# A two-layer graph network on one core: the second group's input is transposed a stage earlier, and its operand sums move to GpSimd

## The chip, the cores and the metric

One core of one Trainium2 chip runs the whole program. The metric is the device time of one execution in microseconds; a kernel's time is the median of its runs. Five engines work in order, each through its own list of instructions, and meet at semaphores: TensorE (PE in the profile; its weight loads are PEld), VectorE (DVE), ScalarE (ACT), GpSimd (POOL) and SyncE (SP), which issues all the DMAs of this kernel.

## The reference

`x` is 128 batches of 128 nodes with 512 features, `adj` a 128x128 matrix, all in float32. Two layers follow each other, a graph convolution and a masked attention with 8 heads, each on a normalised, rectified input and each added to its input.

```
h = max(layernorm(x), 0)
x = x + norm_adj @ (h @ weight) + bias          # norm_adj = adj scaled by its row sums
h = max(layernorm(x), 0)
q, k, v = h @ Wq + bq, h @ Wk + bk, h @ Wv + bv   # 8 heads of 64
scores = q k^T / 8 + (1 - adj) * -1e9
x = x + (softmax(scores) v) @ Wo + bo
```

## The kernel before

**Groups and slots.** The 128 batches are worked on in 32 groups of four (`GB = 4`, `NG = 32`). Time is cut into slots t = 0, 1, 2, ... In slot t, after a hand-written prologue, five products of 512x512 weights follow each other on PE, each called by a letter: W (the convolution weight of group t+1), Q, K and V of group t, and Y (the output weight of group t-1). So the first slot has Q, K, V of group 0 alone, and the slot after it W of group 2, Q, K, V of group 1 and Y of group 0. This document is about V of slot 0 to V of slot 1.

**A product.** The rows of a product are the 512 rows of a group, cut into a 2x2 of blocks like the weight. Seven block products take the place of eight (a Strassen-Winograd form), so a letter has seven steps, 0 to 6. Their left operands are A11, A12, S1, A22, S2, S3, S4; A11, A12, S1 and A22 are first written as the four blocks of the input, and `Operands.combine` (L381 to L384) forms S3, S1, S2 and S4 from them: four 128x512 additions, one after the other. From group 1 on, each of three or four block products is again done by seven smaller ones ("inner"), for which `combine_one` (L94) does nine further 128x256 additions on the operand, and nine on the weight. Three operand tiles exist: `op_a` (op_mix), `op_h` (op_norm) and `op_o` (op_att). The four banks of PSUM `a`, `d`, `b`, `c` hold the block products. Step 0 and 3 write bank a, step 1 bank d, step 2 bank b, step 4 banks b and d, step 5 bank a, step 6 banks b and c; two pieces of bank c are left over for steps 1 and 2 of the next letter. DVE (L448, L463) and ACT (L788, L802) read the banks out, and PE can't write a bank again before that.

**The plan.** What is not one of these products is placed by hand: `at(slot, place, function, ...)` says ahead of which step ("Q1"), after its first part ("Q1b") or after both parts ("Q1c") a piece of work is issued. The order in the program is the order on each engine, so a place decides what stands in front of what on every engine that the piece uses.

**The pieces that matter here.** `norm_h` (L351, ACT) normalises a batch, `transpose_h` turns it by 16 short PE matmuls (L742) and copies the result into the operand (L743, ACT); half 0 of a group (batches 0 and 1) fills A11 and A12, half 1 fills S1 and A22. `attention_operands` is `Operands.combine` on `op_h`. For attention, `row_max` (L850, DVE), `exponentials` (L858, ACT, four or eight heads a call) and `softmax_end` (L865 on DVE, then L870 on POOL, or L868 on ACT for batches 2 and 3 of group 0) follow each other; batch 3 gets its mask apart by `add_mask` (L846, POOL). `split_att` (L875, ACT) writes an attention matrix as two planes of 16-bit words into the buffer of the batch before it and sends it to memory (L876, SP), `turn_att` (L879, SP) brings it back transposed; `transpose_att` does the same on PE (L886). `ln1` and `gcn_norm` prepare the convolution input of group 3 in slot 1 (statistics L332/L333 on DVE, scale L337 to L340 on POOL, L351 on ACT), and `gcn_mix` multiplies it by the graph matrix on PE (`pa`).

**The first round of the weights.** In slots 0 and 1 the weights' own sums are made on POOL and written to memory for later slots (`keep_w`, L205, SP). The value weight lies in the tile `op_o` for that time. Its sums end in slot 1; then it is written out, then the output weight is loaded into the same tile (`load_w`, L201), summed (L282, L94) and written out, and only then may the attention output of group 0 be copied into the tile (L908, ACT). From slot 2 on weights only come back from memory.

The two entries of the plan that say which engine sums the operand of group 1, and which softmax step uses which engine, read:

```
op_h[g].combine(nc.vector if g < 2 else nc.gpsimd, g > 0, within=nc.gpsimd)
if g == 1 or g == 0 and b >= 2:   # ACT, else POOL
```

Of the kernel before, what the change touches and what calls it, by code (L numbers as in the profile page):

```python
# [97 lines left out]
def kernel(  # L98
# [16 lines left out]
    nc = tc.nc  # L115
    B, N, D = x.shape
    P = 128
    H = 8
# [3 lines left out]
    NG = B // GB  # L122
# [269 lines left out]
    op_mix, op_norm, op_att = (Operands(f"op_{k}") for k in "aho")  # L392
# [249 lines left out]
    scale1, op_a, op_h, op_o = {}, {}, {}, {}  # L642
# [123 lines left out]
        nc.sync.dma_start_transpose(out=blocks, in_=h_dram[half].rearrange("n z f -> (n z) f"))  # L766

    def attention_operands(g):
        op_h[g].combine(nc.vector if g < 2 else nc.gpsimd, g > 0, within=nc.gpsimd)

    def attention_residual(g, half):
        add_bias(xts[g, half], bo_bc, engine=nc.gpsimd if g else nc.vector)
# [153 lines left out]
    def at(slot, place, f, *args):  # L926
        plan.setdefault((slot, place), []).append((f, *args))

    for t in range(-1, NG + 1):
# [3 lines left out]
        if 0 <= t - 1 < NG - 1:  # L933
            g = t - 1

            for first, final, place, f, *args in (
                ("W1", "-Y6", "W5", turn_att, 0),
                ("W4b", "-Y6b", "W1b", split_att, 1),
                ("W5", "-Y3", "W2", exponentials, 2, 0, H // 2),
                ("W6", "-Y4", "W3", exponentials, 2, H // 2, H),  # L940
                ("Q2c", "-Y5b", "W4b", softmax_end, 2),
                ("Q1", "-Y5", "W5", exponentials, 3, 0, H // 2),
                ("Q2", "-Y6", "W6", exponentials, 3, H // 2, H),
                ("Q0", "Q1", "Q0", turn_att, 1),
                ("Q4b", "Q0b", "Q0b", softmax_end, 3),
                ("Q4b", "Q0b", "Q3b", split_att, 2),
                ("Q6b", "Q2", "Q5b", split_att, 3),
                ("K1", "Q2", "K0", turn_att, 2),
                ("K3", "Q5", "K2", turn_att, 3),
            ):  # L950
                place = first if t == 1 else final if last else place
                if f in (split_att, turn_att) and turned_in_place(g, args[0]):
                    continue
                at(t - place.startswith("-"), place.strip("-"), f, g, *args)
            if t == 1:
                at(1, "K3", transpose_att, g, 2)
                at(1, "K5", transpose_att, g, 3)
            elif last:
                at(t, "K1", transpose_att, g, 3)
            for b in (2, 3, 0, 1):  # L960
                at(t, "V0", attend, g, b)
        if t == 0:

            at(0, "Q0b", ln2, 1, 0)
            at(0, "Q1b", ln2, 1, 1)
            at(0, "K6", norm_h, 1, 0)
            at(0, "K6", norm_h, 1, 1)
            at(1, "W0", transpose_h, 1, 0)
            at(1, "W0", norm_h, 1, 2)
            at(1, "W1", transpose_h, 1, 1)  # L970
            at(1, "W1", norm_h, 1, 3)
            at(1, "W2", transpose_h, 1, 2)
            at(1, "W3", transpose_h, 1, 3)
            at(1, "W4b", attention_operands, 1)
            at(2, "Q5", attention_residual, 1, 0)
            at(2, "K1", attention_residual, 1, 1)
        elif 1 <= t + 1 < NG and t >= 0:
            g = t + 1
            at(t, "K0b" if g < NG - 1 else "Q0b", ln2, g, 0)
            at(t, "K6b" if g < NG - 1 else "Q3b", ln2, g, 1)  # L980
            if g == NG - 1:

                places = ("Q3", "Q4", "Q5", "Q5", "Q6", "Q6", "K1", "K2", "K2")
                steps = ((norm_h, 0), (norm_h, 1), (transpose_h, 0), (norm_h, 2), (transpose_h, 1), (norm_h, 3))
                steps += ((transpose_h, 2), (transpose_h, 3))
            else:
                places = ("K6", "K6", "V0b", "V1c", "V1c", "V2", None, None, "Y5")
                steps = ((norm_h, 0), (norm_h, 1), (norm_h, 2), (norm_h, 3), (split_h, 2), (split_h, 3))
                for half in range(2):
                    at(t, ("V1", "V2b")[half], write_h, g, half)  # L990
                    at(t, ("V5", "Y1b")[half], turn_h, g, half)
            for place, (f, b) in zip(places, steps):
                at(t, place, f, g, b)
            at(t, places[8], attention_operands, g)
            at(t + 1, "Q3", attention_residual, g, 0)
            at(t + 1, "Q4", attention_residual, g, 1)
# [6 lines left out]
        if 2 <= t + 2 < NG:  # L1003
            g = t + 2
# [11 lines left out]
        if 0 <= t < NG:  # L1016
            g = t
            for b in (0, 1, 3, 2):
                at(t, "V0", scores, g, b)
            if t > 0:  # L1020
                at(t, "V0", output_operands, t - 1)
                for b in range(2 if t < NG - 2 else 0):
                    at(t, "V0", split_h, t + 1, b)
            at(t, "V1b", row_max, g, 0)
            at(t, "V3b", exponentials, g, 0, 0, H // 2)
            at(t, "V4b", exponentials, g, 0, H // 2, H)
            at(t, "V6", softmax_end, g, 0)
            if last:
                at(t, "V5b", row_max, g, 1)
                at(t, "V5b", exponentials, g, 1, 0, H // 2)  # L1030
                at(t, "V6", exponentials, g, 1, H // 2, H)
                at(t, "Y1b", softmax_end, g, 1)
                at(t, "Y2", transpose_att, g, 0)
                at(t, "Y4", transpose_att, g, 1)
            else:
                if t > 0:
                    at(t, "V3b", row_max, g, 1)
                    at(t, "Y1", exponentials, g, 1, 0, H // 2)
                    at(t, "Y2", exponentials, g, 1, H // 2, H)
                    at(t, "Y4", softmax_end, g, 1)  # L1040
                else:
                    at(t, "V4b", row_max, g, 1)
                    at(t, "V5b", exponentials, g, 1, 0, H // 2)
                    at(t, "V6", exponentials, g, 1, H // 2, H)
                    at(t + 1, "W1b", softmax_end, g, 1)
                at(*((t, "Y3b") if t > 0 else (1, "W1")), split_att, g, 0)
                at(t, "V6b", row_max, g, 2)
                at(*((t, "Y1") if t > 0 else (1, "W0")), add_mask, g, 3)
                at(*((t, "Y3b" if g == NG - 2 else "Y6b") if t > 0 else (1, "W6b")), row_max, g, 3)
        if last:  # L1050
            g = t
            at(t, "Y0", row_max, g, 2)
# [64 lines left out]
    def prologue():  # L1117
# [64 lines left out]
        at(0, "K2", keep_w, "q")  # L1182
        at(0, "V1", combine_inner, "v", nc.gpsimd, range(4))
        at(0, "V5", combine_inner, "v", nc.gpsimd, (4, 5))
        at(1, "W0", combine_inner, "v", nc.gpsimd, (6, 7, 8))
        at(1, "W0", keep_w, "v")
        at(1, "W0", load_w, "o", wo, op_att.t)
        at(0, "V0", combine_inner, "k", nc.gpsimd)
        at(1, "Q3c", combine_w, "o", nc.gpsimd)
        at(1, "Q5", combine_inner, "o", nc.gpsimd)  # L1190
        at(1, "K3", keep_w, "o")
        at(1, "W0", output_bias)
        at(1, "K1c", attention_residual, 0, 0)
        at(1, "K2c", attention_residual, 0, 1)

# [66 lines left out]
```

## Time and profile before

| What | us |
|---|---|
| median of 3 runs (2200.32 to 2201.76) | 2201.11 |
| the profiled execution | 2200.75 |
| its span, first to last instruction | 2199.0 |
| PE busy | 2186.2 |
| POOL busy | 1886.1 |
| DVE busy | 1774.9 |
| ACT busy | 1393.8 |

The profiled execution's time is 1.75 us more than its span, and 0.36 us under the median. In the profile's windows of 55 us PE is busy for 52.11, 51.65 and 53.24 us in the first three, and for the whole of each one from 165 us to 2100 us; the last 99 us have 94.18. The granted clock is 0.97 in the window from 55 to 110 us and 1.00 in all others. In the timeline of PE, V of slot 0 begins at 74.96 us, W of slot 1 at 89.27, Q at 105.40, K at 121.01, the attention products at 137.05, V at 144.41 and Y at 155.10.

A line of a timeline has the start in us, the length in us, engine, line of the code, operation, output tile and input tiles, shapes and count, and in brackets the idle time before it with the instruction that ended it. Lengths overlap a little from one instruction to the next, so the distance between starts is what a row costs in a run of such rows.

### The profile page before, as it was taken

The page shows a single profiled execution, that of the slowest core. Times are in us where ns is not written, and L with a number is a line of the kernel's source. Part 1 is how long each engine was busy: PE and PEld are TensorE (multiplying, and loading weights), DVE is VectorE, ACT ScalarE, POOL GpSimd, SP SyncE. Part 2 cuts the span into 40 slices and gives each one's busy share as a digit, 9 for nine tenths or more (in the row PEclk, how much of TensorE's full clock was granted, in tenths as well). Part 3 has the DMA queues.
Part 4 walks back from the last instruction along what each step waited for, and adds up shares of the span by engine and source line. Part 5 has one row for each costly group of instructions (what it writes and reads, how often), then busy time and mean ns, then how long its engine had stood idle before and what let it go on. Part 6 is the DMA issues. An engine that isn't in the chain of part 4 may idle for free.

```text
span 2199.0 us, 77713 instructions
## 1 busy us (share of the span) xinstructions
PE 2186.2 (99%) x31749; PEld 1879.6 (85%) x31749; DVE 1774.9 (81%) x4244; ACT 1393.8 (63%) x3604; POOL 1886.1 (86%) x2049
## 2 busy tenths in 40 slices
PE   9999999999999999999999999999999999999999
PEld 7788888888888888888888888888888888888887
DVE  7777888878888778888788887788877888878876
ACT  4577665765666666666656676566666565765654
POOL 7988988898889898888988898888889888998754
PEclk9999999999999999999999999999999999999999
DMA  5489999999999999999999999999999999999982
GB/s 165 173 260 289 290 293 292 256 284 307 263 288 287 259 297 280 293 296 244 294 312 262 294 271 269 302 286 276 290 259 289 293 279 298 263 276 298 263 261 84
DMA packets 530613, 595.48 MB, mean 271 GB/s; under 512 B 389073, under 2 KB 396369, under 8 KB 529745
## 3 DMA queue, kind: packets, MB, share of 16 engines
q1 hardware_dynamic: 530256, 590.50, 90.6%
q8 instruction: 251, 4.11, 0.8%
q14 instruction: 106, 0.86, 0.1%
HBM read 358.68 MB, written 137.89 MB: 226 GB/s over the span
## 4 chain that ended last, share of the span: by engine, by line
PE 97%; DVE 1%; issue 0%; POOL 0%; DMA 0%; ACT 0%; SPq 0%; POOLq 0%; DVEq 0%; ACTq 0%
PE bank_a L140 37%; PE bank_d L140 22%; PE bank_b L140 11%; PE bank_c L140 11%; PE pa L140 5%; PE bank_d L831 3%; PE po L901 3%; PE pss L831 1%; PE bank_b L901 1%; PE bank_a L901 1%; PE bank_b L831 1%; PE paT L886 0%; DMA xt<-in_x_dram 0%; DVE xt L448 0%; POOL w L282 0%
## 5 line engine op out<-in xcount | busy, mean ns | idle before, releaser
L858 ACT ACTIVATE att<-att,nmx 128x128 f32<-128x128 f32 x1024 | 396.1, 393 | 0.5 <-DVE nmx L850 0.5
L140 PE MATMUL bank_a<-op_h,w 128*64 128x256 f32 x2976 | 353.5, 380 | 0.0
L870 POOL TENSOR_TENSOR att<-att,rsm 128x1024 f32<-128x1024 f32 x122 | 231.7, 1900 | 110.8 <-DVE rsm L865 98.3
L875 ACT COPY att<-att 128x2048 uint16<-128x2048 uint16 x121 | 229.2, 1894 | 114.6 <-POOL att L870 114.5
L448 DVE TENSOR_TENSOR xt<-xt,bank_d 128x512 f32<-128x512 f32 x610 | 270.3, 468 | 11.0 <-PE bank_d L140 0.5
L140 PEld LDWEIGHTS bank_a<-op_h,w 128*64 128x64 f32 x2976 | 207.9, 137 | 81.6 <-issue 0.5
L140 PE MATMUL bank_d<-op_h,w 128*64 128x128 f32 (+1 forms) x3424 | 221.7, 275 | 0.1
L94 POOL TENSOR_TENSOR op_o<-op_o 128x256 f32<-128x256 f32 x297 | 212.4, 739 | 10.1
L788 ACT ACTIVATE q<-bank_a,bqk 128x256 f32<-128x256 f32 x192 | 79.8, 466 | 211.5 <-PE bank_a L140 211.3
L94 POOL TENSOR_TENSOR op_a<-op_a 128x256 f32<-128x256 f32 x279 | 198.5, 734 | 9.6
L94 POOL TENSOR_TENSOR op_h<-op_h 128x256 f32<-128x256 f32 x270 | 191.2, 733 | 11.5 <-DVE op_h L384 2.1
L140 PEld LDWEIGHTS bank_d<-op_h,w 128*64 128x64 f32 x3424 | 195.0, 137 | 7.1 <-POOL w L282 0.5
L858 ACT ACTIVATION_READ_ACCUMULATOR att<-att,nmx 128x1 f32 x1024 | 196.6, 192 | 0.0
L140 PE MATMUL bank_a<-w,op_o 128*64 128x256 f32 x1536 | 182.2, 379 | 0.0
L140 PE MATMUL bank_a<-w,op_h 128*64 128x256 f32 x1488 | 178.0, 381 | 0.0
L140 PE MATMUL bank_a<-w,op_a 128*64 128x256 f32 x1488 | 176.5, 379 | 0.0
L463 DVE TENSOR_TENSOR xt<-bank_a,xt 128x512 f32<-128x512 f32 x252 | 166.8, 683 | 3.1 <-PE bank_a L140 3.1
L850 DVE TENSOR_REDUCE nmx<-att 128x8 f32<-128x1024 f32 x128 | 154.9, 1210 | 0.0
L356 POOL TENSOR_TENSOR xt<-xt,b_o 128x1024 f32<-128x1024 f32 x62 | 147.2, 2376 | 0.0
L140 PEld LDWEIGHTS bank_a<-w,op_o 128*64 128x64 f32 x1536 | 107.5, 137 | 41.2
L351 ACT ACTIVATE h<-op_o,nb,rs 128x512 f32<-128x512 f32 x112 | 91.8, 820 | 76.2 <-POOL nb L340 76.2
L140 PEld LDWEIGHTS bank_a<-w,op_h 128*64 128x64 f32 x1488 | 102.4, 137 | 43.7
(188 smaller groups left out, 5779.8 us busy)
## 6 DMA issues: line engine op xcount, KB each, us to landing
w<-wd_v SPq DMA_DIRECT2D x155, 512.0 KB, 4.9
w<-wd_o SPq DMA_DIRECT2D x155, 512.0 KB, 9.0
w<-wd_q SPq DMA_DIRECT2D x150, 512.0 KB, 8.3
w<-wd SPq DMA_DIRECT2D x145, 512.0 KB, 5.3
planes<-att SPq DMA_DIRECT2D x121, 512.0 KB, 6.3
out_dram<-xt SPq DMA_DIRECT2D x62, 512.0 KB, 7.4
planes_h<-q SPq DMA_DIRECT2D x58, 512.0 KB, 3.2
op_o<-in_x_dram SPq DMA_DIRECT2D x56, 512.0 KB, 9.8
```

The source lines that it names most:

```text
L94: engine.tensor_tensor(twice(out), twice(x), twice(y), ALU.subtract if minus else ALU.add)
L140: nc.tensor.matmul(out[y : y + P // 2], lhsT[:, y : y + P // 2], rhs, **flags)
L351: nc.scalar.activation(h, src[:, j, :], AF.Relu, bias=nb[:, j : j + 1], scale=rs[:, j : j + 1])
L356: engine.tensor_tensor(t, src, bias.unsqueeze(1).to_broadcast([P, t.shape[1], D]), ALU.add)
L448: nc.vector.tensor_tensor(dst, dst, src, f)
L463: nc.vector.tensor_tensor(t, src.rearrange("p (r f) -> p r f", r=2), t, ALU.add)
L831: nc.tensor.matmul(pss[p][:, c, :], qs[g][rows, c, cols], ks[g][rows, c, cols], start=True, stop=True)
L850: nc.vector.tensor_reduce(nmx, att_of(g, b), AX.X, ALU.max, negate=True)
L858: nc.scalar.activation(att[:, h, :], att[:, h, :], AF.Exp, bias=nmx[:, h : h + 1], scale=1.0, accum_out=sm[:, h : h + 1])
L870: nc.gpsimd.tensor_tensor(att, att, rsm.unsqueeze(2).to_broadcast([P, H, P]), ALU.mult)
L875: nc.scalar.copy(planes, halves)
L901: nc.tensor.matmul(po[p * HD : (p + 1) * HD, c * P : (c + 1) * P], vs[g][:, b, h * HD : (h + 1) * HD], aT[:, p * NC + c, :], start=True, s ...
```

## The change

Within slots 0 and 1, for groups 0 and 1, pieces are put elsewhere in the plan; and the four block sums of `op_h` for group 1 are done by POOL instead of DVE. No other slot is touched.

- `transpose_h` of batches 0 and 1 of group 1 and `norm_h` of batches 2 and 3 go from W0 and W1 to V4 and V5 of slot 0; `transpose_h` of batches 2 and 3 from W2 and W3 to W0 and W1; `attention_operands(1)` from W4b to W1b.
- The last three sums of the value weight, its `keep_w` and the load of the output weight go from W0 to W2, so behind the operand sums on POOL.
- The mask of batch 3 goes from W0 to W3, its row maximum from W6b to Q1b. `softmax_end` of batches 0 and 1 of group 0 goes from V6 and W1b to W3c and W6c.
- The exponentials of batches 1, 2 and 3 and the two `split_att` (W1 to Q0c, W4b to Q1c) move behind; so do the `softmax_end` of batches 2 and 3 (to Q4c and K0c), the `turn_att` of batches 0 and 1 (to Q1 and Q2) and `output_bias` (to W0c).

```diff
     def attention_operands(g):
-        op_h[g].combine(nc.vector if g < 2 else nc.gpsimd, g > 0, within=nc.gpsimd)
+        op_h[g].combine(nc.vector if g < 1 else nc.gpsimd, g > 0, within=nc.gpsimd)
...
-                ("W1", "-Y6", "W5", turn_att, 0),
-                ("W4b", "-Y6b", "W1b", split_att, 1),
+                ("Q1", "-Y6", "W5", turn_att, 0),
+                ("Q1c", "-Y6b", "W1b", split_att, 1),
                 ("W5", "-Y3", "W2", exponentials, 2, 0, H // 2),
                 ("W6", "-Y4", "W3", exponentials, 2, H // 2, H),
-                ("Q2c", "-Y5b", "W4b", softmax_end, 2),
-                ("Q1", "-Y5", "W5", exponentials, 3, 0, H // 2),
-                ("Q2", "-Y6", "W6", exponentials, 3, H // 2, H),
-                ("Q0", "Q1", "Q0", turn_att, 1),
-                ("Q4b", "Q0b", "Q0b", softmax_end, 3),
+                ("Q4c", "-Y5b", "W4b", softmax_end, 2),
+                ("Q2c", "-Y5", "W5", exponentials, 3, 0, H // 2),
+                ("Q3c", "-Y6", "W6", exponentials, 3, H // 2, H),
+                ("Q2", "Q1", "Q0", turn_att, 1),
+                ("K0c", "Q0b", "Q0b", softmax_end, 3),
...
-            at(1, "W0", transpose_h, 1, 0)
-            at(1, "W0", norm_h, 1, 2)
-            at(1, "W1", transpose_h, 1, 1)
-            at(1, "W1", norm_h, 1, 3)
-            at(1, "W2", transpose_h, 1, 2)
-            at(1, "W3", transpose_h, 1, 3)
-            at(1, "W4b", attention_operands, 1)
+            at(0, "V4", transpose_h, 1, 0)
+            at(0, "V4", norm_h, 1, 2)
+            at(0, "V5", transpose_h, 1, 1)
+            at(0, "V5", norm_h, 1, 3)
+            at(1, "W0", transpose_h, 1, 2)
+            at(1, "W1", transpose_h, 1, 3)
+            at(1, "W1b", attention_operands, 1)
...
-            at(t, "V6", softmax_end, g, 0)
+            at(*((t, "V6") if t > 0 else (1, "W3c")), softmax_end, g, 0)
...
-                    at(t, "V5b", exponentials, g, 1, 0, H // 2)
-                    at(t, "V6", exponentials, g, 1, H // 2, H)
-                    at(t + 1, "W1b", softmax_end, g, 1)
-                at(*((t, "Y3b") if t > 0 else (1, "W1")), split_att, g, 0)
+                    at(t + 1, "W2", exponentials, g, 1, 0, H // 2)
+                    at(t + 1, "W3", exponentials, g, 1, H // 2, H)
+                    at(t + 1, "W6c", softmax_end, g, 1)
+                at(*((t, "Y3b") if t > 0 else (1, "Q0c")), split_att, g, 0)
                 at(t, "V6b", row_max, g, 2)
-                at(*((t, "Y1") if t > 0 else (1, "W0")), add_mask, g, 3)
-                at(*((t, "Y3b" if g == NG - 2 else "Y6b") if t > 0 else (1, "W6b")), row_max, g, 3)
+                at(*((t, "Y1") if t > 0 else (1, "W3")), add_mask, g, 3)
+                at(*((t, "Y3b" if g == NG - 2 else "Y6b") if t > 0 else (1, "Q1b")), row_max, g, 3)
...
-        at(1, "W0", combine_inner, "v", nc.gpsimd, (6, 7, 8))
-        at(1, "W0", keep_w, "v")
-        at(1, "W0", load_w, "o", wo, op_att.t)
+        at(1, "W2", combine_inner, "v", nc.gpsimd, (6, 7, 8))
+        at(1, "W2", keep_w, "v")
+        at(1, "W2", load_w, "o", wo, op_att.t)
...
-        at(1, "W0", output_bias)
+        at(1, "W0c", output_bias)
```

On POOL the order from 91 us on becomes: four block sums and nine inner sums of `op_h`, three sums of the value weight, the mask (L846), `softmax_end` of batch 0, then of batch 1 (L870), the scale of `ln1` of group 3 (L337 to L340), the sums of the output weight. On ACT, after the first step of Q: `split_att` of batch 0, the read of bank d (L788), `split_att` of batch 1, four exponentials of batch 3, the normalisation of the first batch of group 3 (L351), the read of bank a, four exponentials, the second L351, the scaling of batch 2 (L868), then the third L351.

## The prediction

> **What bounds the kernel now.** I read the page first, then the waits of PE, then the timelines of all five engines between V of slot 0 (74.96 us) and V of slot 1 (144.41 us), which is all that the change moves.
>
> ```profile
> PE 2186.2 (99%) x31749; PEld 1879.6 (85%) x31749; DVE 1774.9 (81%) x4244; ACT 1393.8 (63%) x3604; POOL 1886.1 (86%) x2049
> ```
>
> PE is busy for all but 12.8 us of 2199.0, so whatever moves PE here moves the end by as much. Of PE's idle time only three waits lie where the change works. The timeline of PE has them:
>
> ```profile
> 88.25 1.10 PE L314 MATMUL pb<-att 128*128 128x512 f32 x2 [0.53 <-DVE rsm L865]
> 103.21 0.70 PE L140 MATMUL bank_b<-w,op_a 128*64 128x128 f32 x4 [2.82 <-DVE xt L448]
> 116.39 1.09 PE L140 MATMUL pa<-ant,h 128*64 128x128 f32 x16 [1.76 <-ACT h L351]
> ```
>
> The windows of one microsecond show what the second one costs besides (the last three columns are the granted clock, the DMA share and GB/s):
>
> ```profile
> 103.00:104.00 1.00, 0.79 (x8) 0.79 (x10) 0.90 (x3) 1.00 (x7) 1.00 (x2) 0.59 0.86 369
> 104.00:105.00 1.00, 1.00 (x14) 1.00 (x12) 0.97 (x4) 1.00 (x6) 1.00 (x3) 0.50 0.77 328
> 105.00:106.00 1.00, 1.00 (x10) 0.81 (x8) 1.00 (x3) 0.52 (x4) 1.00 (x2) 0.50 0.10 41
> 106.00:107.00 1.00, 1.00 (x10) 0.58 (x8) 1.00 (x4) 0.00 (x0) 0.92 (x3) 0.70 0.00 0
> ```
>
> Clocks of 0.59, 0.50, 0.50 and 0.70 lose 1.7 us more. The wait of 2.82 is DVE's: it does the four sums of op_h ahead of reading PE's banks, one of them stretched beside POOL:
>
> ```profile
> 98.77 2.27 DVE L382 TENSOR_TENSOR op_h<-op_h 128x512 f32<-128x512 f32 x1
> ```
>
> The timelines of POOL, ACT and SP give the durations that I use below:
>
> ```profile
> 91.64 1.89 POOL L870 TENSOR_TENSOR att<-att,rsm 128x1024 f32<-128x1024 f32 x1
> 93.50 2.39 POOL L846 TENSOR_TENSOR att<-att,msk 128x1024 f32<-128x1024 f32 x1
> 95.84 2.35 POOL L94 TENSOR_TENSOR op_o<-op_o 128x256 f32<-128x256 f32 x3
> 98.14 2.35 POOL L870 TENSOR_TENSOR att<-att,rsm 128x1024 f32<-128x1024 f32 x1
> 102.64 6.59 POOL L94 TENSOR_TENSOR op_h<-op_h 128x256 f32<-128x256 f32 x9 [2.14 <-DVE op_h L384]
> 163.94 1.28 POOL L381 TENSOR_TENSOR op_h<-op_h 128x512 f32<-128x512 f32 x1
> 169.38 6.61 POOL L94 TENSOR_TENSOR op_h<-op_h 128x256 f32<-128x256 f32 x9
> ```
>
> ```profile
> 100.52 1.90 ACT L875 COPY att<-att 128x2048 uint16<-128x2048 uint16 x1 [2.78 <-POOL att L870]
> 113.19 2.44 ACT L868 ACTIVATE att<-att,rsm 128x128 f32<-128x128 f32 x8 [0.62 <-DVE rsm L865]
> 115.54 0.80 ACT L351 ACTIVATE h<-xt,nb,rs 128x512 f32<-128x512 f32 x1
> 138.55 1.07 ACT L908 COPY op_o<-po 128x512 f32<-128x512 f32 x2 [1.67 <-DMA wd_o<-op_o]
> ```
>
> ```profile
> 98.22 0.34 SPq L205 DMA_DIRECT2D wd_v<-op_o  x1
> 107.20 1.91 SPq L201 DMA_DIRECT2D op_o<-in_L_gnn_Wo_dram  x4
> 129.01 0.32 SPq L205 DMA_DIRECT2D wd_o<-op_o  x1
> ```
>
> The four block sums on POOL take 5.44 us (163.94 to 169.38), the nine inner ones 6.6. The last ACT line already waits for a chain through SP and POOL (value weight out, output weight in, sums, out), which PE does not feel yet.
>
> **The gain: three waits go.** PE without waits: V ends at 87.10 us, plus two groups of 16 transposes at 0.44 (the step from 91.05 to 91.50) is 87.99. Third transposes 0.44, W0 1.75, bias product 1.02 (88.25 to 89.27), so the fourth transposes start at 91.2 and W1 at 91.64. The normalised batches are there (ACT: 82.61 plus four exponentials at 0.385, copy 0.89, L351 0.71, is done at 85.9; the next at 89.0). W1 to W6 are 1.53, 0.88, 1.73, 1.96, 1.73, 1.10: Q starts at 100.57 instead of 105.40. DVE without its four sums has read bank d by 96.1 (W2 ends at 94.25, five reads at 0.33 to 0.38; W4 needs it at 96.2) and bank b by 97.75 (W6 needs it at 99.47). Q0 to Q4 are 1.73, 1.96, 1.09, 1.73, 1.97, so the first mix `pa` could start at 109.05 instead of 116.39: 7.3 us gained.
>
> **What stands against it: POOL's order.** The fourth batch is copied by ACT at 92.9, so POOL starts the block sums at 93.0: 5.44 and 6.6 give 105.04; three value sums 2.3 (95.84 to 98.14), 107.34; mask 2.35, 109.7; first L870 1.86, 111.55; second, 113.4. The operand itself is in time: Q1 reads its fifth inner sum (98.44 plus 5 at 0.735 is 102.1) at 103.0, Q2 the seventh at 104.9 (done 103.6). Who waits for the rest:
> - DVE: the row maximum of batch 3 stands in front of all reads of Q and waits for the mask: 109.8, then 1.13, statistics 0.82, so the read of bank b (0.33) is done at 112.1. Q4 wanted that bank at 107.1: PE stands.
> - ACT: `split_att` of batch 0 waits for the first L870 at 111.55 and holds back the read of bank d: 1.8 (the L875 step from 94.03 to 95.83) and 0.73, 114.1. DVE's reads behind it (0.33, 0.2, 0.33) let Q4's matmuls start at 115.1 instead of 107.5.
> - ACT further: second split 1.8, four exponentials 1.54, 117.45; L351 to PE's start took 0.85 (115.54 to 116.39), so `pa` starts at 118.3, against 116.39: **1.9 us later than before**, the 7.3 given back and more.
> - Then the second L351 (0.73 for bank a, 1.54, 0.85): `pa` 2 at 121.3 (before 119.04). The scaling of batch 2 now waits for DVE's reads (119.0 plus 2.65, reciprocal 0.2) and stands in front of the third L351: 121.9, 2.34, copy 0.46, reads 0.73, 0.85, so `pa` 3 at 126.3 (before 122.73): 3.6 later. Scaling of batch 3 from 128.45 to 130.8 stands in front of the copies that free the two small banks for `paT`: second half at 132.6, 0.51, K3 at 133.1 (before 128.66): **4.45 later**.
>
> **The chain through memory.** The value weight goes out at 107.35 instead of 98.22; 8.98 later the output weight is issued (98.22 to 107.20), its last part 1.5 later, at 117.9. Landing of this tile's DMAs runs from 2.8 to 9.4, the four loads 4.2 in the middle, the last in the row 5.1; I take 4.7: 122.6 (bounds 120.7 and, by the longest, 127.3). Sums 5.3 and 7.35 (121.63 to 128.97), 135.3. SP has by then passed both splits and their transposes (the second issued at about 131.7 to 133.6). Write-out to ACT's start took 9.54 (129.01 to 138.55): 144.85. Four copies at 0.49 and 0.1 for the handover free banks b and a at 146.9. PE would reach the second score product at 141.64 plus 4.45, 146.1, and waits until 146.95: **5.3 later**, my value. Cover removed: before, ACT waited 1.67 there at no cost to PE. The transposed read-back of batch 1 lands 3.9 to 5.8 after its issue, up to 137.5, so the write-out shares the DMA engines for up to 3 us, which I price at 0 to 3 more and take at 0 (the nearest row, at 129.01, had a quiet queue).
>
> **After that** nothing is left to lose or to win: the value weight's last parts are issued some 6 us later, 11.1 to landing, about 149, and V2 is due at 153; POOL, 6.3 us later than before (135.3 against 128.97), starts the sums of the attention output at 151.2, has the fifth inner one at 160.3, and Y1 wants it at 162.1 (156.83 plus 5.3). PE has no further wait up to 2100 us, so the delay stays. Moved at no cost: the mask, row maxima and exponentials themselves (same instructions, same count; ACT idles from 103.2 to 111.55), the two SP transposes (due at the attention products at 144). They cost only through what stands behind them, priced above.
>
> **The clock.** The row shows half clock after an idle time of 2.99 us (100.22 to 103.21) and none after 1.99 (114.4 to 116.39). Here PE idles 5.0 and, after eight matmuls of Q4, 2.6 us more; its 28 matmuls then take up to 3.06 instead of 1.53 and end at 118.2, just under the 118.3 of `pa`: 0, bound 1.5.
> The Trainium skill, "TensorE: Matmul & The Clock Gate" (section "Part 1: The HAM clock gate"), puts the drop at an idle window of about 3.4 us, free-running, and a cold stretch of about as long. By it the old wait of 2.99 need not have dropped the clock, though it did; the new first gap surely would. By the rule this change buys a longer cold stretch than it removes, which would add at most those 1.5 us.
>
> The sum: without waits PE is at the second score product 7.3 us earlier (134.3), the chains put it at 146.95, 12.6 after that: -7.3 and +12.6 make +5.3. On the profiled execution that is a span of 2204.3 and 2206.05 us; the median of the runs lies 0.36 above it, so **2206.4 us**. 0.2% is 4.4 us, about what a measurement of this kernel can tell from no change.
>
> **Rivals.**
> - *The waits go and nothing takes their place*: -7.3, 2193.8 us. For it: DVE's and PE's side of the sum. Against: the mask would have to end by about 105.5, and POOL has 16.7 us to do from 93.0. It decides if POOL's thirteen op_h sums took 8 us instead of 12. Chance 0.05.
> - *Given back in part*: the first stall stays (+1.9), the later ones (third L351, `paT`, copies of op_o) are partly covered: +1.9 to +4.3, taken as +3.5, 2204.6 us. For it: before, the same ACT steps had slack; the output weight may land by 120.7 and one POOL row of 1.60 among the nine L94 was chance. Chance 0.25.
> - *The memory chain decides alone*: the write-out of the output weight shares the DMA engines with the transposed read-back: +8.3, 2209.4 us. For it: a DMA share of 1.0 and more whenever a transpose runs (117 to 122 us). Against: the read-back may be over by 136. Decides if the write-out takes over 11 us. Chance 0.2.
> - *Forecast*: +5.3, its own range +4.4 to +7, 2205.5 to 2208.1. Chance 0.5.
>
> **Numbers.** Faster 0.05 (first rival), same 0.25 (second), slower 0.7 (the other two). Range: from +1.4 (the ACT chain alone, 0.5 early) to +10.4 (8.3 with 0.6 for a stretched POOL row and 1.5 for the clock): 2202.5 to 2211.5.
>
> **What would show it.** No wait of PE at the bias product and in W6, Q starting near 100.6; PE waiting in Q4 for DVE, first at bank b and then at bank d, DVE's L850 waiting for POOL's L846 until about 109.7, ACT's L875 waiting for L870 until about 111.6; `pa` at 118.3, 121.3 and 126.3; ACT's first L908 released by wd_o at about 144.9. I am wrong if POOL passes the mask before 106, or if the second score product starts before 145.

## The result and the profile after

Seven runs of the changed kernel have a median of 2207.85 us (2206.43 to 2211.35), against 2201.11 before: a ratio of 1.0032, interval 1.0021 to 1.0044. The change makes the kernel 6.7 us slower; 6.4 of it can be pointed at in the trace, as follows.

The page says that PE's work is the same and that its idle time grew: the span of the profiled execution is 2206.4 (before 2199.0), PE's busy time

```profile
PE 2188.1 (99%) x31749; PEld 1879.8 (85%) x31749; DVE 1768.6 (80%) x4240; ACT 1394.4 (63%) x3604; POOL 1891.3 (86%) x2053
```

so 18.3 us idle instead of 12.8, and 1.9 more of busy time for the same matmuls. The timeline of PE shows where (start, duration, line, operation, and in brackets the idle time before it and what ended it):

```profile
101.62 1.89 PE L140 MATMUL bank_a<-op_h,w 128*64 128x256 f32 x16
...
113.17 0.69 PE L140 MATMUL bank_b<-op_h,w 128*64 128x128 f32 x8 [4.87 <-DVE q L448]
...
116.20 3.26 PE L140 MATMUL bank_d<-op_h,w 128*64 128x128 f32 x28 [2.33 <-DVE q L448]
119.25 1.67 PE L140 MATMUL pa<-ant,h 128*64 128x128 f32 x16
...
127.23 1.09 PE L140 MATMUL pa<-ant,h 128*64 128x128 f32 x16 [0.89 <-ACT h L351]
...
148.40 0.49 PE L831 MATMUL bank_b<-k,q 64*128 64x128 f32 x2 [0.91 <-ACT op_o L908]
...
151.76 1.95 PE L140 MATMUL bank_a<-w,op_h 128*64 128x256 f32 x16
```

The three old waits are gone: no wait is listed at the bias product, in W6 or at the first `pa`, and Q starts at 101.62. This execution ran 0.91 late already when the change begins (its V step of slot 0 that stood at 80.19 starts at 81.10, after a longer wait in the prologue), so Q is at 100.71 in the old frame, 4.7 earlier than before. All of it and more is given back in Q4, where PE stands twice, and again at the second score product. POOL's timeline has the reason for the first:

```profile
94.00 1.28 POOL L381 TENSOR_TENSOR op_h<-op_h 128x512 f32<-128x512 f32 x1 [1.43 <-ACT op_h L743]
...
99.45 6.59 POOL L94 TENSOR_TENSOR op_h<-op_h 128x256 f32<-128x256 f32 x9
106.00 2.34 POOL L94 TENSOR_TENSOR op_o<-op_o 128x256 f32<-128x256 f32 x3
108.30 2.34 POOL L846 TENSOR_TENSOR att<-att,msk 128x1024 f32<-128x1024 f32 x1
110.59 3.75 POOL L870 TENSOR_TENSOR att<-att,rsm 128x1024 f32<-128x1024 f32 x2
...
123.71 5.21 POOL L282 TENSOR_TENSOR op_o<-op_o 128x512 f32<-128x512 f32 x4 [3.73 <-DMA op_o<-in_L_gnn_Wo_dram]
129.00 8.31 POOL L94 TENSOR_TENSOR op_o<-op_o 128x256 f32<-128x256 f32 x9
```

POOL takes its work in order without a gap from 94.00 to 114.3, and DVE and ACT each stand behind one piece of it. First DVE, then ACT:

```profile
110.67 1.22 DVE L850 TENSOR_REDUCE nmx<-att 128x8 f32<-128x1024 f32 x1 [4.92 <-POOL att L846]
```

```profile
112.52 1.90 ACT L875 COPY att<-att 128x2048 uint16<-128x2048 uint16 x1 [8.12 <-POOL att L870]
...
146.78 1.07 ACT L908 COPY op_o<-po 128x512 f32<-128x512 f32 x2 [4.22 <-DMA wd_o<-op_o]
```

The row maximum waits 4.92 for the mask, and with it the reads of PE's banks; `split_att` waits 8.12 for the first L870, and with it the reads and the normalisation that `pa` needs. At 146.78 ACT stands again, for the write-out of the output weight. Its issue is in SP's timeline:

```profile
128.92 0.38 SPq L876 DMA_DIRECT2D planes<-att  x1
135.11 1.88 SPq L879 DMA_TRANSPOSE att<-planes  x1
137.34 0.33 SPq L205 DMA_DIRECT2D wd_o<-op_o  x1
```

The write-out goes out at 137.34, just behind two things: POOL's sums, which end at 137.31, and SP's transposed read-back of batch 1, which ends at 136.99. (The sums took 8.31 here and 7.35 before.)

The clock paid too. In the windows of one microsecond (the third number from the end is the granted clock) PE is cold from the first wait to the first `pa`:

```profile
113.00:114.00 1.00, 0.69 (x8) 0.45 (x8) 0.35 (x2) 1.00 (x1) 1.00 (x1) 0.83 1.53 655
114.00:115.00 1.00, 0.00 (x0) 0.00 (x0) 0.00 (x0) 1.00 (x3) 0.83 (x3) 0.50 0.78 328
...
119.00:120.00 1.00, 1.00 (x14) 0.80 (x12) 0.05 (x1) 1.00 (x4) 0.88 (x3) 0.50 0.68 178
120.00:121.00 1.00, 1.00 (x16) 0.92 (x14) 1.00 (x3) 1.00 (x7) 0.00 (x0) 0.76 0.90 209
```

### The profile page after: what moved, and what is told of

It is laid out like the page before. It is cut to its first block, busy times and chain, and to the rows that moved or that the text cites. A ratio compares the mean times of both kernels' runs of the same rounds, so it can differ in the third digit from the quotient of the medians.

```text
span 2206.4 us, 77715 instructions
## 1 busy us (share of the span) xinstructions
PE 2188.1 (99%) x31749; PEld 1879.8 (85%) x31749; DVE 1768.6 (80%) x4240; ACT 1394.4 (63%) x3604; POOL 1891.3 (86%) x2053
## 4 chain that ended last, share of the span: by engine, by line
PE 96%; POOL 2%; DMA 1%; DVE 1%; issue 0%; ACT 0%; SPq 0%; POOLq 0%; ACTq 0%; DVEq 0%
PE bank_a L140 37%; PE bank_d L140 22%; PE bank_b L140 11%; PE bank_c L140 11%; PE pa L140 5%; PE bank_d L831 3%; PE po L901 2%; PE pss L831 1%; PE bank_b L901 1%; PE bank_a L901 1%; PE bank_b L831 1%; POOL op_o L94 0%; DMA wd_o<-op_o 0%; DMA xt<-in_x_dram 0%; DMA op_o<-in_L_gnn_Wo_dram 0%
## 5 line engine op out<-in xcount | busy, mean ns | idle before, releaser
L870 POOL TENSOR_TENSOR att<-att,rsm 128x1024 f32<-128x1024 f32 x122 | 231.2, 1896 | 109.6 <-DVE rsm L865 103.0
L448 DVE TENSOR_TENSOR xt<-xt,bank_d 128x512 f32<-128x512 f32 x610 | 269.4, 466 | 11.0 <-PE bank_d L140 0.4
L94 POOL TENSOR_TENSOR op_o<-op_o 128x256 f32<-128x256 f32 x297 | 213.4, 742 | 10.1
L788 ACT ACTIVATE q<-bank_a,bqk 128x256 f32<-128x256 f32 x192 | 80.0, 467 | 212.4 <-PE bank_a L140 212.4
L94 POOL TENSOR_TENSOR op_a<-op_a 128x256 f32<-128x256 f32 x279 | 198.4, 734 | 9.6
L94 POOL TENSOR_TENSOR op_h<-op_h 128x256 f32<-128x256 f32 x270 | 191.2, 733 | 9.4
L356 POOL TENSOR_TENSOR xt<-xt,b_o 128x1024 f32<-128x1024 f32 x62 | 147.3, 2377 | 0.0
L351 ACT ACTIVATE h<-op_o,nb,rs 128x512 f32<-128x512 f32 x112 | 91.8, 820 | 76.4 <-POOL nb L340 76.4
```

Of the source, the lines that this page charges most:

```text
L94: engine.tensor_tensor(twice(out), twice(x), twice(y), ALU.subtract if minus else ALU.add)
L351: nc.scalar.activation(h, src[:, j, :], AF.Relu, bias=nb[:, j : j + 1], scale=rs[:, j : j + 1])
L356: engine.tensor_tensor(t, src, bias.unsqueeze(1).to_broadcast([P, t.shape[1], D]), ALU.add)
L448: nc.vector.tensor_tensor(dst, dst, src, f)
L870: nc.gpsimd.tensor_tensor(att, att, rsm.unsqueeze(2).to_broadcast([P, H, P]), ALU.mult)
```

## Two stretches that split every run

Two marks in PE's timeline split the disturbed part and take the start of each execution out of it. Stretch A runs from that V step of slot 0 (80.19 before) to the start of K3 (128.66 before); it holds the stalls in Q and at `paT`. Stretch B runs from K3 to V of slot 1 (144.41 before); it holds the score products. The last column is the median against that of the kernel before, run beside it on the same chip.

| kernel | A | B | A+B against before | median against before |
|---|---|---|---|---|
| before | 48.47 | 15.75 | 0 | 0 |
| changed | 53.25 | 17.41 | +6.44 | +6.74 |
| e1, value sums back | 51.75 | 15.75 | +3.28 | +3.49 |
| e2, block sums on DVE | 50.82 | 18.65 | +5.25 | +4.88 |
| e3, mask first | 51.80 | 20.80 | +8.38 | +8.65 |
| e4, write-out in two | 53.23 | 15.76 | +4.77 | +4.73 |
| e5, L870 on ACT | 48.45 | 15.76 | -0.01 | +0.18 |
| e6, all untied | 42.86 | 17.53 | -3.83 | -3.97 |
| e7, residual additions later | 53.25 | 17.52 | +6.55 | +6.67 |
| e9, read-back behind | 53.25 | 30.70 | +19.73 | +20.47 |
| e8, both | 53.25 | 29.30 | +18.33 | +19.83 |
| e10, read-back just behind | 53.24 | 19.79 | +8.81 | +8.89 |

In all but e8 and e9 the two stretches account for the time to within 0.4, so nothing after V of slot 1 adds more than that. (The profiled execution of e8 is 1.3 under its median; that of e9 came 0.7 later to the V mark than the kernel before.) So the loss of 6.44 is 4.78 in A and 1.66 in B, and each experiment can be read by which of the two it moves.

## The experiments

Each edits the changed kernel unless it says otherwise. e4 and e6 have a line of code more near the top, so their L449, L352 and L909 are L448, L351 and L908 of the others.

**e1: the value weight's sums, its write-out and the load behind it go back to where they were.**

```diff
-        at(1, "W2", combine_inner, "v", nc.gpsimd, (6, 7, 8))
-        at(1, "W2", keep_w, "v")
-        at(1, "W2", load_w, "o", wo, op_att.t)
+        at(1, "W0", combine_inner, "v", nc.gpsimd, (6, 7, 8))
+        at(1, "W0", keep_w, "v")
+        at(1, "W0", load_w, "o", wo, op_att.t)
```

> The changed kernel, with one piece put back: the last three sums of the value weight, its write-out and the load of the output weight stand again at W0, ahead of the operand sums on POOL. Reference point: the changed kernel, 2207.85 us, in whose trace the mask (L846) ends at 110.6, the second L870 at 114.3, the first pa of Q5 starts at 119.25 and V of slot 1 at 151.76. My theory (POOL's order sets it, through DVE, ACT and then the chain through memory): the sums fit into 1.4 us of POOL idle time and 0.95 of delay, so the operand sums start at 95.0, the mask ends at 109.3, the second L870 at 113.0, pa starts 1.3 earlier (117.9); the memory chain begins 13 us earlier and no longer holds ACT's L908, which takes away another 1.7: 2204.9 us (2203.9 to 2206.2). Rival 'the memory chain alone is the loss': back to before or under it, 2201 us or less. Rival 'DVE's wait for the mask is the loss and the memory chain nothing': 1.3 less, 2206.5.

Measured: 2204.88 us, ratio 1.0016 (1.0007 to 1.0025). B is back at 15.75: the write-out is issued at 130.03, and neither ACT's first L908 nor the score product waits for it. A falls by 1.5, since POOL then reaches the mask and the two L870 that much earlier. PE's timeline:

```profile
110.59 0.66 PE L140 MATMUL bank_b<-op_h,w 128*64 128x128 f32 x8 [3.38 <-DVE q L448]
```

The wait of 4.87 is 3.38. The chain through memory is worth 1.66, and A stays 3.3 over before without it.

**e2: the four block sums of `op_h` go back to DVE, at their new, early place.**

```diff
-        op_h[g].combine(nc.vector if g < 1 else nc.gpsimd, g > 0, within=nc.gpsimd)
+        op_h[g].combine(nc.vector if g < 2 else nc.gpsimd, g > 0, within=nc.gpsimd)
```

> The changed kernel with the four block sums of op_h for group 1 back on DVE, at their new place W1b. My theory: DVE does them from 94.0 to 96.8, which makes W4 wait some 1.8 us on PE, but PE waits in Q4 anyway; POOL is free 2.7 us earlier for all that follows, so the mask ends at 107.9, the second L870 at 111.6, pa starts at 116.6, the output weight's write-out starts 2.7 earlier: 2205.2 us (2204.0 to 2206.5). Rival 'the engine of the four sums is the whole loss': 2201 or less. Rival 'the order behind the sums is the whole loss, the engine nothing': 2207.9.

Measured: 2206.27 us, ratio 1.0022 (1.0013 to 1.0031), about 1 above what was expected. A falls by 2.4, to 50.82; four sums of 1.28 off POOL bring its L870 forward, and DVE pays with short waits of PE in W4 (0.90 and 0.24). But B grows by 1.2. PE comes to the score product 2.4 earlier, the write-out (issued at 134.27, 2.3 earlier in this frame) took 10.6 to ACT's start instead of 9.4 (why is not shown), so that the copies are only 1.2 earlier:

```profile
146.47 0.49 PE L831 MATMUL bank_b<-k,q 64*128 64x128 f32 x2 [2.15 <-ACT op_o L908]
```

**e3: the mask is put in front of the sums on POOL, at W0.**

```diff
-                at(*((t, "Y1") if t > 0 else (1, "W3")), add_mask, g, 3)
+                at(*((t, "Y1") if t > 0 else (1, "W0")), add_mask, g, 3)
```

> The changed kernel with the mask of batch 3 (L846, POOL) alone put back to W0, ahead of the operand sums. My theory: the row maximum on DVE waits for nothing any more and PE's first gap in Q4 (4.87 us at bank b) goes; but ACT still waits for the first L870, which ends 1.3 us earlier (111.2), and pa is set by ACT: 118.0. The value weight's sums come 1.0 later, so the write-out and ACT's L908 come 1.0 later, and that decides the end: 2208.9 us (2207.3 to 2210.3), no gain from a gap of 4.9 us taken away. Rival 'PE's longest wait, DVE behind the mask, is the loss': 4.9 us less, 2203.0.

Measured: 2210.04 us, ratio 1.0039 (1.0025 to 1.0053), no faster than the change itself: 8.65 over the kernel before, where the change has 6.74. PE's timeline:

```profile
114.58 3.26 PE L140 MATMUL bank_d<-op_h,w 128*64 128x128 f32 x28 [5.93 <-DVE q L448]
...
148.54 0.49 PE L831 MATMUL bank_b<-k,q 64*128 64x128 f32 x2 [2.66 <-ACT op_o L908]
```

The longest wait of the changed kernel, 4.87 for bank b, is gone, and the next wait takes it over with 5.93: bank d's read stands behind ACT's `split_att`, which still waits for L870 behind all of POOL's sums. A falls by 1.45 only, which is what the first L870 starts earlier, so that longest wait was not the one that set the end. PE then stands 2.66 for the write-out and the clock drops behind that wait (0.50 from about 149.6 to 153.1), which makes B 20.80, 3.4 more.

**e4: the write-out as two DMAs, the first with 16 of its 40 slots, those that ACT's L908 overwrites first.**

```diff
-        nc.sync.dma_start(w_dram[name], w_sb[name].t)
+        for some in (slice(0, 16), slice(16, SLOTS)) if name == "o" else (slice(0, SLOTS),):
+            nc.sync.dma_start(w_dram[name][:, some, :], w_sb[name].t[:, some, :])
```

> The changed kernel with the write-out of the output weight (keep_w of o) issued as two DMAs, the 16 slots into which ACT's L908 writes first. My theory: L908 then waits for 1 MB instead of 2.5 MB and its 4.2 us wait for the write-out goes, so V of slot 1 starts at 150.1 instead of 151.76: 2206.2 us (2205.2 to 2207.3). Rival 'the memory chain alone is the loss': 2202 or less. Rival 'the memory chain is hidden': 2207.9.

Measured: 2206.12 us, ratio 1.0022 (1.0013 to 1.0032). SP's and ACT's timelines:

```profile
136.62 1.01 SPq L206 DMA_DIRECT2D wd_o<-op_o  x2
```

```profile
143.40 1.07 ACT L909 COPY op_o<-po 128x512 f32<-128x512 f32 x2 [2.01 <-DMA wd_o<-op_o]
```

Both parts go out directly behind the read-back, no earlier than before, but ACT's first copy starts 6.8 after the issue instead of 9.4. A is unchanged at 53.23, B is 15.76, and no wait is left at the score product: the 1.66 alone.

**e5: e1, and the softmax scaling of batches 0 and 1 of the first group (L870 on POOL) done by ACT (L868).**

```diff
-        if g == 1 or g == 0 and b >= 2:
+        if g <= 1:
```

> The kernel of e1 (value sums back at W0; 2204.88 us, first pa of Q5 at 116.67) with the two L870 of group 0 taken off POOL: softmax_end of batches 0 and 1 scales on ACT (L868), which is idle there from 98.9 to 102.5 and from 103.2 to 109.9 in e1. My theory (ACT behind POOL's L870 sets pa): ACT has both matrices scaled by 103.6, split_att waits for nothing, the read of bank d is done by 106.9; what is left is DVE behind the mask (until 109.2) and the scale of ln1 behind it: Q4's matmuls start at about 112 instead of 113.62 and pa at 113.3 to 114.9 instead of 116.67: 2202.5 us (2201.0 to 2203.9). Rival 'what is left of the loss is DVE behind the mask alone': no change, 2204.9. Rival 'ACT is full, 4.7 us more work on it cost as much': 2206 to 2209.

Measured: 2201.53 us, ratio 1.0001 (0.9992 to 1.0010): level with before. PE's timeline:

```profile
111.68 0.66 PE L140 MATMUL bank_b<-op_h,w 128*64 128x128 f32 x8 [3.15 <-DVE q L448]
112.78 1.75 PE L140 MATMUL bank_d<-op_h,w 128*64 128x128 f32 x28 [0.44 <-DVE q L448]
114.36 1.04 PE L140 MATMUL pa<-ant,h 128*64 128x128 f32 x16
```

The wait for the mask stays (3.15), the one behind L870 shrinks from 2.37 in e1 to 0.44, and A is 48.45. So the two L870 at the end of POOL's queue, with ACT behind them, are worth 3.3 of A. e1, e2 and e3 say the same: after the V mark their first L870 starts at 28.01, 27.06 and 28.05, where the changed kernel has 29.49, so 1.48, 2.43 and 1.44 earlier, and A is 1.50, 2.43 and 1.45 shorter, whether the wait for the mask stays (3.38 in e1) or is gone (e3).

**e6: every tie loosened.** e1 and e4 together, batch 0's scaling alone on ACT, and the steps of ACT, POOL and SP placed behind what they wait for:

```diff
-        if g == 1 or g == 0 and b >= 2:
+        if g == 1 or g == 0 and b != 1:
...
-                ("Q1c", "-Y6b", "W1b", split_att, 1),
+                ("Q6c", "-Y6b", "W1b", split_att, 1),
...
-                ("Q2", "Q1", "Q0", turn_att, 1),
-                ("K0c", "Q0b", "Q0b", softmax_end, 3),
+                ("K0", "Q1", "Q0", turn_att, 1),
+                ("K3c", "Q0b", "Q0b", softmax_end, 3),
...
-                    at(t + 1, "W6c", softmax_end, g, 1)
+                    at(t + 1, "Q2", softmax_end, g, 1)
...
-                at(*((t, "Y1") if t > 0 else (1, "W3")), add_mask, g, 3)
+                at(*((t, "Y1") if t > 0 else (1, "Q1c")), add_mask, g, 3)
...
```

Left out are the moves of the same kind: `softmax_end` of batch 0 to W6c and of batch 2 to Q1c, the exponentials of batch 3 to K1c and K2c, the row maximum of batch 3 to Q5, `transpose_att` of batch 3 to K6.

> A version made from what e1 to e4 showed: the kernel of e1 with the write-out of the output weight in two parts, batch 0 of group 0 scaled on ACT (W6c), the scale of ln1 on POOL ahead of mask and L870 (mask at Q1c, softmax_end of batch 1 at Q2), the row maximum of batch 3 at Q5, its exponentials at K1c and K2c, softmax_end of batch 2 at Q1c and of batch 3 at K3c, split_att of batch 1 at Q6c, its turn_att at K0, transpose_att of batch 3 at K6. My theory: the transposes' early place is worth 7.3 us once nothing of the next steps stands behind POOL's sums; pa starts at 109 to 109.5 (116.4 before), PE has no wait over 1 us up to V of slot 1, and the time is 2195.5 us (2194.0 to 2198.5), under both kernels. Rival 'the gain is not there, POOL as a whole sets the pace of slot 1': 2201 to 2204, with PE waiting for L282/L94 of the output weight or for ACT's L908. Rival 'ACT takes over as the bound': waits of PE for L351 or for L670 of 3 us and more in all, 2199 to 2202.

Measured: 2197.38 us, ratio 0.9981 (0.9972 to 0.9990): faster than both kernels, 4.0 below before and some 10.5 below the change. PE's timeline:

```profile
108.84 1.75 PE L140 MATMUL bank_d<-op_h,w 128*64 128x128 f32 x28 [0.89 <-DVE q L449]
110.90 1.09 PE L140 MATMUL pa<-ant,h 128*64 128x128 f32 x16 [0.31 <-ACT h L352]
...
129.51 0.66 PE L140 MATMUL bank_c<-op_h,w 128*64 128x128 f32 x8 [1.55 <-DVE k L449]
```

The first `pa` starts at 110.90 where before it started at 116.39, and the waits that are left sum to 2.75 us. One of them is the 1.55 in K, longer than the 1 us that was expected at most, and B has grown by 1.8. The early places kept their gain up to Q, which starts 20.5 after the V mark (25.2 before, 20.5 in the changed kernel); in the changed kernel the orders behind them ate it. How much of the 4.0 those looser orders would have won with the pieces in their old places was not run.

**e7: the two additions of the output bias (L356 on DVE) moved out of the output weight's nine inner sums.** It asks why these sums took 8.31.

```diff
-        at(1, "K1c", attention_residual, 0, 0)
-        at(1, "K2c", attention_residual, 0, 1)
+        at(1, "K4c", attention_residual, 0, 0)
+        at(1, "K5c", attention_residual, 0, 1)
```

> The changed kernel with its two additions of the output bias to the residual (L356 on VectorE, 128x1024 each) moved from K1c and K2c to K4c and K5c, so that they no longer lie beside the nine inner sums of the output weight on GpSimd. Theory (each L356 beside these sums stretches one of them by about 0.9: nine took 6.6 with none, 7.35 with one, 8.31 with two): the nine sums take 6.6 to 6.7, the L356 1.2 each instead of 1.71 and 1.25, the write-out is issued about 1.6 earlier than 137.34, the first L908 starts near 145.1 and the wait of 0.91 before the second score product goes: 2206.9 (2206.0 to 2207.9). Rival (the stretch comes from elsewhere, such as the DMA traffic or the bank reads of VectorE that stay beside the sums): the nine sums still take 8 or more, the wait of 0.91 stays, 2207.9.

Measured: 2207.44 us, ratio 1.0031 (1.0019 to 1.0044); A 53.25, B 17.52, both as in the changed kernel. The nine sums by line, first in the changed kernel, then in e7 (shortest, median and longest in ns):

```profile
L94 POOL TENSOR_TENSOR op_o<-op_o x9: 717/728/1707, 129.0 to 136.6; 128x256 f32<-128x256 f32 x9
```

```profile
L94 POOL TENSOR_TENSOR op_o<-op_o x9: 724/729/733, 127.7 to 133.4; 128x256 f32<-128x256 f32 x9
```

With no L356 beside them all nine take 0.73 and the sums 6.47: the stretch is the two L356. Yet nothing was gained: the write-out went out 0.3 earlier after the V mark, not 1.6 as expected. SP's timeline of e7 says why:

```profile
134.11 1.75 SPq L879 DMA_TRANSPOSE att<-planes  x1
135.97 0.52 SPq L205 DMA_DIRECT2D wd_o<-op_o  x1
```

The sums end at 134.17, and SP issues the write-out at 135.97, directly behind the read-back. The write-out had two walls that ended within 0.4 of each other. With the first one gone the second holds, and the first L908 starts 65.8 after the V mark, where it started at 65.7. The additions met POOL's sums again in their new place (L384, 1.28 elsewhere, took 2.15 beside one, and L356 1.54 and 1.65), and DVE's reads behind them cost PE 0.70 ahead of the score product, in time that it would have waited there.

**e9, e8 and e10: the read-back behind the write-out.** e9 moves only the read-back, in the plan's list of the first group's steps; e8 does so too and moves the additions (K3c and K4c); e10 is e8 with the read-back directly behind the write-out.

```diff
-                ("Q2", "Q1", "Q0", turn_att, 1),
+                ("K4", "Q1", "Q0", turn_att, 1),
```

> The changed kernel with only the transposed read-back of batch 1 (L879 on SP) moved from Q2 to K4, behind the write-out of the output weight. Theory of two walls: the nine sums still take about 8.3 beside the two L356, the write-out is issued as they end, at most 0.3 earlier than in the changed kernel, and the wait before the second score product stays within 0.5 of 0.91: 2207.8 (2207.2 to 2208.5). Rival (SP's read-back alone held the write-out): issued 1 or more earlier, 2206.8.

> The changed kernel with both walls in front of the write-out taken away: the two additions of the output bias (L356 on VectorE) go from K1c and K2c to K3c and K4c, away from the nine inner sums of the output weight, and the transposed read-back of batch 1 (L879 on SP) goes from Q2 to K4, so that SP issues the write-out of the output weight ahead of it. Theory (the write-out had two walls that ended within 0.3 of each other, GpSimd's stretched sums at 137.3 and SP's read-back at 137.0, so that taking one away gains nothing): the sums take about 6.5, the write-out is issued about 2 earlier than in the changed kernel, the first L908 starts about 1.7 to 2.1 earlier, PE no longer waits for the copies at the second score product (0.91, and 0.6 more between its two banks), with up to 0.7 given back by later bank reads of VectorE: 2206.8 (2206.0 to 2207.5). Rival (the sums alone decide): the same gain as with the additions moved alone, 2207.4 or more. Rival (the end of K is not what sets the time): 2207.9.

> As e8 (the two L356 at K3c and K4c), with the transposed read-back of batch 1 issued directly behind the write-out of the output weight at K3, and so ahead of the loads L1088 that wait for the write-out, where in e8 it stood behind them. Theory (two walls in front of the write-out): sums about 6.5, the write-out issued as they end, 2 earlier than in the changed kernel; the read-back ends its issue about 0.4 earlier than there and PE does not wait for it; the first L908 starts 1 to 1.9 earlier than in the changed kernel (1.9 if the read-back beside it costs the write-out nothing, 1 if it shares the DMA engines with it), the waits for the copies at the second score product shrink from 0.91 to 0 to 0.3, up to 0.7 is given back by later bank reads of VectorE: 2206.8 (2206.0 to 2207.6). Rival (the read-back beside it stretches the write-out by all that is won): the first L908 where it was, 2207.9.

Measured: 2221.48 (ratio 1.0093, 1.0079 to 1.0107), 2220.84 (1.0091, 1.0077 to 1.0105) and 2210.02 (1.0036, 1.0022 to 1.0050). All three times miss the expectations; the queue of SP in e8 and e10 says where:

```profile
134.38 0.33 SPq L205 DMA_DIRECT2D wd_o<-op_o  x1
134.76 2.67 SPq L1088 DMA_DIRECT2D w<-wd_v  x3
143.92 2.39 SPq L1088 DMA_DIRECT2D w<-wd_o  x5
146.35 7.94 SPq L879 DMA_TRANSPOSE att<-planes  x1
```

```profile
135.37 0.32 SPq L205 DMA_DIRECT2D wd_o<-op_o  x1
135.78 8.64 SPq L879 DMA_TRANSPOSE att<-planes  x1
```

In e8 and e9 the read-back fell behind the loads that wait for the write-out, an order I had not looked at, and PE waits 11.8 and 13.1 for it at the attention product. In e10 it follows the write-out at once, takes 8.64 on the queue itself, and PE waits 2.19 for it and runs cold behind that (0.50 from about 148.1 to 151.5). What they do show is the wall: in e8 the write-out goes out 0.03 after its sums end (134.35), and the first L908 starts at 144.00, 63.7 after the V mark, against 65.7 in the changed kernel, 2 earlier. In e9, where the sums keep their 8.32, it starts 0.5 earlier. (In e10 one of the two additions came to lie beside the sums again; they took 7.43, and the first L908 starts 0.9 earlier.) To gain by that the write-out would have to pass the read-back without delaying it, which no run here does; e4 leaves the order and shortens what ACT waits for.

## Why the prediction was right, and where it was off

The three waits that go, Q's new start, POOL's order and both places where PE would stand came as worked out; in the new frame (add 0.91) the first `pa` was due at 119.2 and came at 119.25, the third at 127.2 and came at 127.23.

- *The waits and Q.* Q was put at 100.57, 101.48 in this frame, and came at 101.62. That this gain can reach the end is shown by e6.
- *POOL's order.* Mask end 109.7 and first L870 end 111.55 were 110.64 and 112.5: right with the offset. e5 shows that L870 with ACT behind it carries 3.3 of A, and e1 and e3 together that DVE's wait for the mask, though longer in the row, does not set the end.
- *Stretch A.* +4.45 was predicted and +4.78 measured. The third `pa` is on time; the second half of `paT` came at 133.76 instead of 133.5, K3 0.3 late. The clock's cold stretch, taken at 0 with a bound of 1.5, made the first `pa` slow (1.67), and the second started 0.3 late; by the third, ACT's order had covered it. How long it lasts did not matter: in e4, e9 and e10 it is 10.2 instead of 6.8 long, as it begins inside the wait, and A is the same to 0.02.
- *Stretch B.* Here a size failed: +0.85 was predicted (PE at 146.1, held until 146.95) and +1.66 measured. The write-out was due at 135.3, 136.2 in this frame, and went out at 137.34. Two steps failed together, and either alone would have done most of it. "Sums 5.3 and 7.35" carried over a row that had one L356 beside it; this place has two, and each adds about 0.9 (6.47 with none, 7.35 with one, 8.31 with two). And "SP has by then passed both splits and their transposes (the second issued at about 131.7 to 133.6)" was wrong: from the issue of batch 1's planes to the read-back passed 6.2 (128.92 to 135.11) where before it was 3.9 (117.58 to 121.52), and SP was in the read-back until 136.99, 136.1 in the old frame. The write-out itself took 9.44 to ACT's start (9.54 before), so nothing for shared DMA engines, as taken; over the runs in which ACT waits for it as one DMA it took 9.1 to 10.6.
- *The sum.* +5.3 was predicted and +6.44 measured in the two stretches; the other 0.9 of the profiled span is the start of that execution, which lies between 79.94 and 81.10 in the profiled runs here.
- *The rivals.* No wait in place of the old ones: refuted by both walls. Given back in part: refuted, as all of A's later stalls came. The write-out stretched by the read-back beside it: not in this kernel. e10, which puts them side by side, shows that the read-back suffers (8.64) and the write-out does not (9.4).

Left open: the changed kernel's runs spread over 4.9 us and the old one's over 1.4. The slowest has a mean granted clock of 0.997, the six others 0.998, which fits more cold time; no experiment addressed that.

## What to carry to other kernels

Taking waits away in front of an engine that works in order is worth only what the next thing in line allows: list for each queue what the moved work pushes back, and who stands behind that, as three sums of 2.3 us together here set an output copy 40 us later. The longest wait in the row need not be the one to remove; follow what ends last behind it (e3 removed 4.87, and stretch A fell by 1.45). And where two events end close together in front of a transfer, removing one proves little (e7): look at the queue as well as at the data.

## What the hardware showed that was not expected

**A transposed read-back is slow behind a large transfer.** It took 1.7 to 2.3 us on SP's queue in every other place in this stretch, but 8.64 directly behind the write-out of 2.5 MB (e10), and 7.94 and 7.92 behind five loads of 512 KB (e8, e9). Whether the queue, a semaphore shared with an earlier transfer or the DMA engines held it was not separated.

**DVE's additions of two tensors stretch POOL's, and can be stretched.** Beside L356 one L94 took 1.707 instead of 0.73. L356 itself took 1.71 and 1.25 beside POOL's sums, so not each one is longer; but L382 on DVE took 2.27 beside POOL's L870 (before) and 0.69 where POOL stood idle (e2). The Trainium skill, "GPSIMD Engine Reference" (section "1. Specifications"), says that GpSimd shares its SBUF interfaces with VectorE and that VectorE instructions with two SBUF inputs contend there; the rows agree. e7 is the test: L356 moved away, and the nine sums ran at 0.73 each.

**The length of an idle time does not tell whether the clock drops.** It fell to 0.50 at idle times of 2.82 (before; the prediction counts it as 2.99), 4.87, 2.66 (e3) and 2.19 (e10), and stayed at 1.0 after 3.15 (e5), 2.36 and 2.15 (e2). In the changed kernel it stayed down from about 113.7 to 120.5, with a second wait of 2.33 inside. By the clock in the profiles, the cold stretches have a step. They last 3.41 us in the kernel before and behind the late waits of e3 and e10, 6.83 in the changed kernel, in e1 and at the first stall of e3, e7 and e8, and 10.24 at that of e4, e9 and e10: once, twice and three times the same length. Nor does the drop keep a fixed distance from the wait: with the same first wait of about 4.87 it came 2.5 us into it in e4, 3.4 in e10, and 0.5 after its end in the changed kernel. The Trainium skill, "TensorE: Matmul & The Clock Gate" (section "Part 1: The HAM clock gate"), has a free-running window of about 3.4 us; the step and the wandering start agree with it. (The prediction's "surely would" for its first gap says more than such a window allows, as a gap of 5 us need not hold a whole one.) But 2.19 is far less than a whole idle window. Counted on that step, the 3.15 of e5 falls on two windows, with 2.0 idle in the first and 1.2 in the second, and the 2.66 of e3 has 2.3 in one; yet the 2.19 of e10 has only 1.9 in one, so the idle share of a window does not settle it alone, and what does stays open.
